# A graph layer on one core: engine order stated for 26 blocks only, an own bank for placed sums, two node banks, and the second block's additions moved up

## The chip, the cores and the metric

The kernel runs on one core of a Trainium2 chip. A core has five engines with a queue each: TensorE (PE, matmuls, with its weight loads shown as PEld), VectorE (DVE), ScalarE (ACT), GpSimd (POOL) and SyncE (SP). They run side by side and wait for each other through semaphores. Matmul results go to PSUM, which this kernel fills to its last bank[...]. The metric is device time in microseconds; lower is better. Times are medians over runs, and one execution was taken by the hardware profiler.

## The reference

A graph of 8192 nodes with 256 channels and 131072 edges with 64 attributes, everything in float32. Edges come sorted by destination. Reduced to what matters:

```python
ea  = edge_attr @ w_e + b_e                      # 131072 x 256
msg = relu(x[src] + ea)                          # a gather of rows of x
agg = segment_sum(msg, dst, 8192)
t   = x + agg
h_local = bn1(relu(t @ w1 + b1) @ w2 + b2 + x)
# attention within each graph of 32 nodes, 4 heads of 64 channels, on x
q, k, v = split(x.reshape(256, 32, 256) @ in_w.T + in_b)
h_attn  = bn2(softmax(q @ k.T / 8) @ v @ out_w.T + out_b + x)
out = h_local + h_attn
out = bn3(out + relu(out @ m_w1 + m_b1) @ m_w2 + m_b2)
return layernorm(x + out)
```

## The kernel before

**Edges** go in 128 blocks of 1024 (`NB`). For a block, `gather` (L124) issues eight indirect DMAs on the POOL queue, each fetching 128 rows of 256 channels into an `xs` tile; four such tiles exist, so the gathers of block b + 2 write the tile that the messages of block b - 2 read. The first `NX` blocks gather from x itself and add the bias `be` by extra matmuls (L468); later ones gather from `xb`, a copy of x with the bias in it, which `copy_load` and `copy_store` make during the first pairs. `load_edges` brings the attributes two blocks at a time. `edge_transpose` turns a block's attributes on TensorE into a `tp` tile, and ScalarE copies that to `eaT` (L169). `edge_products` multiplies `eaT` with `w_e` into two `pe` tiles of two banks each (L460). `edge_messages` adds `xs` to each on VectorE (L482) and takes relu on ScalarE (L486). `edge_hot` makes one-hot rows of the destinations (L491). `edge_sums` sums messages into windows by matmuls with them (`pw`, L505), copied by ScalarE (`ws`, L511). `edge_place` places the windows into node columns by another matmul (`l2`, L523) and VectorE adds the result to the chunk's `xT` (L533).

**Nodes** go in 16 chunks of 512 (`NCH`), and eight blocks feed one chunk. A chunk passes through three generators: `attention_front` (loads, transposes L283, q and k L294), `attention_back` (v L308, scores into two `pe` tiles L326, copied out by ScalarE L336, softmax on VectorE and ScalarE L342 to L353, then `oT` L361 and the output projection L373), and `dense` (four layers L392, transposes back L429, layer norm L434 to L442, store). Their matmuls write `at` tiles of one bank (`bank()`), evacuated by ScalarE or VectorE.

**PSUM** is shared out as three `at` banks, two `pe` tiles of two banks, and one bank with the tag `sm`, which `tp`, `pw` and `l2` use in turn.

**Order.** Blocks go in pairs until the last `NS` = 8, which go singly. Each pair's loop body issues edge steps, and between them calls `work.run(us)`. `Work` holds four streams of generators; a call takes steps from them in turn until the estimates they yield (1.7 for a layer step, 1.8 for scores, and so on) use up the given share of `per`, which is a number of blocks times `PER_X` or `PER`. A yield of `REST` keeps a stream out for the next call. A yield of `BEHIND` keeps it out until a call with `behind=True`, which is the pair's last, half of `per`, issued after the second block's messages: `attention_back` yields it ahead of the scores. Shares a stream can't use are kept only up to 2.0.

The whole edge loop stands in `tc.manual_schedule` (L609) for PE, DVE and ACT: each of these runs its instructions in the order in which the program states them. Outside such a block a planner lays out an engine's order itself when the program is built.

The order of a pair b, b + 1 in the loop: products b, messages b, window sums of the previous pair, products b + 1, node work (0.3 of `per`), the copy of x in early pairs, transposes of b + 2, work (0.1), placing, work (0.1), transposes of b + 3, one-hot rows of both, messages b + 1, work (0.5).

Of the kernel before, what the change touches and what calls it, by code (L numbers as in the profile page):

```python
# [9 lines left out]
FP = mybir.dt.float32  # L10
# [23 lines left out]
BPC = NB // NCH  # L34
TN = CH // P
GT = P // NPG
NX = 18
ND = 2
NS = 8
AGG_ROWS = N + 2 * P  # L40
TE = 8
RS = 1.0 / (1.0 + 1e-5) ** 0.5
LN_EPS = 1e-5

REST, BEHIND = -1.0, -2.0


VECS = ["b1", "b2", "bn1_g", "bn1_b", "in_b", "out_b", "bn2_g", "bn2_b", "m_b1", "m_b2", "bn3_g", "bn3_b"]
# [3 lines left out]
def gnn_kernel(ctx: ExitStack, tc: tile.TileContext, x, src, dst, edge_attr, w, out):  # L52
# [65 lines left out]
    pps = fast.enter_context(tc.tile_pool(name="fast_ps", bufs=1, space=PSUM))  # L118

    def bank():  # L120
        return pps.tile([P, CH], FP, name="at", tag="at", bufs=3)

    def bank2():
        return pps.tile([P, 2, CH], FP, name="pe", tag="pe", bufs=2)  # L124
# [176 lines left out]
    def attention_back(st, pool, bank, bank2):  # L301
        xT, hA, qk = st["xT"], st["hA"], st["qk"]
        vn = pool.tile([P, TN, C], FP, name="vn", tag="vn")
        for t0 in range(0, TN, 2):
            ps = bank()
            for t in range(t0, t0 + 2):
                for k in range(KC):
                    nc.tensor.matmul(  # L308
                        ps[:, (t - t0) * C : (t - t0 + 1) * C],
                        xT[:, k, t * P : (t + 1) * P],  # L310
                        inT[:, k, 2 * C :],
                        start=(k == 0),
                        stop=(k == KC - 1),
                    )
            nc.vector.tensor_copy(vn[:, t0 : t0 + 2, :].rearrange("p t c -> p (t c)"), ps)
            st["v"] = t0 + 2 == TN
            yield 1.7
        yield BEHIND

        pr = pool.tile([P, TN, H, NPG], FP, name="pr", tag="pr")  # L320
        for hh in range(H // 2):
            two = bank2()
            for t in range(TN):
                for s in range(2):
                    a = t * P
                    nc.tensor.matmul(  # L326
                        two[:, s, a : a + P],
                        qk[s * DH : (s + 1) * DH, hh, a : a + P],
                        qk[s * DH : (s + 1) * DH, KC + hh, a : a + P],
                        start=True,  # L330
                        stop=True,
                    )
            two4 = two.rearrange("p s (t k) -> p s t k", t=TN)
            for g in range(GT):
                q = slice(g * NPG, (g + 1) * NPG)
                nc.scalar.copy(pr[q, :, 2 * hh : 2 * hh + 2, :].rearrange("p t s k -> p s t k"), two4[q, :, :, q])  # L336
        st["scores"] = True
        yield 1.8
        prf = pr.rearrange("p t h k -> p (t h k)")
        pr3 = pr.rearrange("p t h k -> p (t h) k")  # L340
        mx = pool.tile([P, TN * H], FP, name="mx", tag="mx")
        nc.vector.tensor_reduce(mx, pr3, AX.X, ALU.max)  # L342
        nc.vector.tensor_sub(pr3, pr3, mx[:, :, None].to_broadcast([P, TN * H, NPG]))
        nc.scalar.activation(prf, prf, AF.Exp, scale=1.0 / DH**0.5)
        yield 0.0
        sm = pool.tile([P, TN * H], FP, name="sm", tag="sm")
        nc.vector.tensor_reduce(sm, pr3, AX.X, ALU.add)
        nc.vector.reciprocal(sm, sm)
        nc.vector.tensor_mul(pr3, pr3, sm[:, :, None].to_broadcast([P, TN * H, NPG]))

        for g in range(GT):
            q = slice(g * NPG, (g + 1) * NPG)
            nc.vector.transpose(bd[q, :, :, g, :].rearrange("p t h q -> p (t h) q"), pr3[q])  # L353
        yield REST
        oT = pool.tile([P, KC, CH], FP, name="oT", tag="oT")
        for k in range(KC):
            ps = bank()
            for t in range(TN):
                for s in range(2):
                    h = 2 * k + s  # L360
                    nc.tensor.matmul(  # L361
                        ps[s * DH : (s + 1) * DH, t * P : (t + 1) * P],
                        vn[:, t, h * DH : (h + 1) * DH],
                        bd[:, t, h].rearrange("p g q -> p (g q)"),
                        start=True,
                        stop=True,
                    )
            nc.scalar.activation(oT[:, k, :], ps, AF.Identity, bias=v_("in_b", 2 * KC + k))
        yield 1.8
        for o in range(KC):  # L370
            ps = bank()
            for k in range(KC):
                nc.tensor.matmul(  # L373
                    ps, outT[:, k, o * P : (o + 1) * P], oT[:, k, :], start=(k == 0), stop=(k == KC - 1)
                )
            nc.vector.scalar_tensor_tensor(
                hA[:, o, :], ps, s2[:, o : o + 1], hA[:, o, :], op0=ALU.mult, op1=ALU.add
            )
            st["done"] = o == KC - 1
            yield 1.7  # L380
# [135 lines left out]

    def edge_place(blocks, ws, oh2):

        l2 = pps.tile([P, KC, C], FP, name="l2", tag="sm", bufs=1)
        last = len(blocks) - 1  # L520
        for i in range(last + 1):
            for k in range(KC):
                nc.tensor.matmul(  # L523
                    l2[:, k, i * NPB : i * NPB + WB], ws[:, i, k * P : (k + 1) * P], oh2[:, i, :],
                    start=(i == 0 and k == 0), stop=(i == last), skip_group_check=True,
                )
        n = blocks[0] * NPB - WL
        end = n + last * NPB + WB
        for c in range(max(n, 0) // CH, (min(end, N) - 1) // CH + 1):
            assert chunk[c]["v"]  # L530
            a, z = max(n, c * CH), min(end, (c + 1) * CH)
            xT = chunk[c]["xT"][:, :, a - c * CH : z - c * CH]
            nc.vector.tensor_add(xT, l2[:, :, a - n : z - n], xT)  # L533
# [22 lines left out]
    class Work:  # L556
# [4 lines left out]

        def __init__(self, n):
            self.streams = [[] for _ in range(n)]
            self.rest, self.behind, self.turn, self.owed = [0] * n, [False] * n, 0, 0.0

        def add(self, stream, ready, gen):
            self.streams[stream].append((ready, gen))

        def may(self, i, behind):
            s = self.streams[i]  # L570
            return s and not self.rest[i] and (behind or not self.behind[i]) and s[0][0]()

        def run(self, us, behind=False):
            self.owed += us
            n, done = len(self.streams), 0
            self.rest = [max(r - 1, 0) for r in self.rest]
            while self.owed > 0:
                turns = [i % n for i in range(self.turn, self.turn + n)]
                i = next((i for i in turns if self.may(i, behind and done > 0)), None)
                if i is None:  # L580
                    i = next((i for i in turns if self.may(i, behind)), None)
                if i is None:
                    break
                if behind:
                    self.behind[i] = False
                t = next(self.streams[i][0][1], None)
                if t is None:
                    self.streams[i].pop(0)
                elif t == REST:
                    self.rest[i] = 2  # L590
                elif t == BEHIND:
                    self.behind[i] = True
                else:
                    self.owed -= t
                    done += t > 0
                    self.turn = (i + 1) % n
            self.owed = min(self.owed, 2.0)

        def finish(self):
            while any(self.streams):  # L600
                self.run(1e9, True)

    BACK, FRONT, DENSE, DENSE2 = range(4)
    work = Work(4)
    PER = 5.4
    PER_X = 4.5
    OTHER = ("vn", "qk", "oT", "pr", "o")
    placed = -1
    with tc.manual_schedule(engines={PE, mybir.EngineType.DVE, mybir.EngineType.Activation}):  # L609

        def last_of(c, t_z=TN):

# [21 lines left out]
        for i, c, t_a, t_z in (  # L634
# [6 lines left out]
                ready = lambda r=ready: r() and chunk[NCH - 1].get("done")  # L641
            work.add(i, ready, d)

        sums, waiting = None, []
        b = 0
        while b < NB:
            n = 2 if b < NB - NS else 1
            blocks, per = range(b, b + n), n * (PER_X if b < NX else PER)
            for i in blocks:
                if i % 2 == 0 and i + 4 < NB:  # L650
# [11 lines left out]
            waiting = list(blocks)  # L662
            if n == 2:
                edge_products(b + 1)
            if b == NB - 1:
                work.run(2.0)
                edge_place(*sums)
                placed = sums[0][-1]
                break
# [12 lines left out]
                    work.run(0.1 * per)  # L682
            for i in blocks:
                edge_hot(i)
            if n == 2:
                edge_messages(b + 1)
            work.run(0.5 * per, True)
            b += n
        edge_hot(NB - 1)
        work.run(1.5, True)  # L690
        sums = edge_sums(waiting)
        work.run(1.0, True)
        edge_place(*sums)
        placed = NB - 1
        work.finish()
# [124 lines left out]
```

## Time and profile before

| | |
|---|---|
| median of 3 runs | 1448.02 us (1444.78 to 1451.0) |
| profiled execution, device time | 1451.19 us |
| its span, first to last instruction | 1449.1 us |
| mean granted TensorE clock | 0.962 |
| gathers (POOL DMA_INDIRECT, three groups) | 1008, 952 to 994 ns each |
| moved by DMA | 206.77 MB, mean 143 GB/s |

How to read it: busy shares are averages over the span. A group's line in the profile gives the source line, the engine, the operation, what it writes and reads, and how often; after the bar stand its busy time, the mean of one, then the idle time of its engine right before it and what ended that idle time. "issue" is time in which an engine waited for nothing that the profile shows. fp32 matmuls appear in the trace as two instructions each.

From 569 to 1280 us the trace repeats one period of 88.5 to 89.2 us with 64 gathers, which is eight blocks and one chunk. Before that lie a start of 46 us with loads and set-up and a stretch in which the dense part has not yet begun or catches up; after it come the eight single blocks and the last dense steps.

In the trace, `pe<-DVE msg` in the list of waits means that PE stood idle before a matmul into a `pe` tile until the additions L482 ended.

### The profile page before, as it was taken

What the parts mean: (1) busy time and instruction counts of PE and PEld (TensorE: products, weight loads), DVE (VectorE), ACT (ScalarE), POOL (GpSimd) and SP (SyncE); (2) the same over time, 40 slices, a digit from 0 to 9 for tenths busy, and PEclk for the clock granted to TensorE, in tenths of its full rate; (3) what the DMA queues carried; (4) which work ended last, traced back from release to release, by engine and by line L of the source; (5) the groups of instructions that cost most, each with busy time, mean ns of one, the idle gap of its engine ahead of it and who ended that gap; (6) DMA issues with size and microseconds to landing.
All of it is one profiled execution on the core that took longest, in us unless ns stands there. A gap on an engine that the chain in (4) does not pass through costs nothing.

```text
span 1449.1 us, 21166 instructions
## 1 busy us (share of the span) xinstructions
PE 1268.8 (88%) x8275; PEld 795.4 (55%) x8275; DVE 709.4 (49%) x1202; ACT 658.3 (45%) x963; POOL 981.6 (68%) x1032
## 2 busy tenths in 40 slices
PE   5898999999999998988969799797997969888977
PEld 4566665555555655555545455454554545545645
DVE  5455635546463645354363543545345354454443
ACT  3434434545454554444444443453534545444433
POOL 7777757777777777775757667576775767757620
PEclk9998999999999999999989999999999999999999
DMA  8868544545454545453444534444444444434410
GB/s 288 293 196 258 184 137 135 164 118 163 134 148 130 162 133 148 127 157 95 134 128 130 158 101 134 137 130 139 124 127 132 135 130 129 135 109 136 118 53 17
DMA packets 140613, 206.77 MB, mean 143 GB/s; under 512 B 19646, under 2 KB 103900, under 8 KB 139740
## 3 DMA queue, kind: packets, MB, share of 16 engines
q0 software_dynamic: 49152, 134.28, 32.4%
q1 hardware_dynamic: 89468, 69.76, 15.3%
q8 instruction: 67, 1.10, 0.3%
q10 hardware_dynamic: 1888, 1.32, 0.3%
q14 instruction: 38, 0.31, 0.1%
HBM read 188.51 MB, written 16.78 MB: 142 GB/s over the span
## 4 chain that ended last, share of the span: by engine, by line
PE 52%; POOL 15%; DVE 14%; issue 9%; ACT 5%; DMA 5%; DVEq 0%; ACTq 0%; POOLq 0%
PE at L392 17%; POOL xs L134 15%; PE pe L460 12%; PE at L294 5%; DVE msg L482 5%; PE pw L505 4%; PE l L523 4%; PE at L373 3%; PE at L308 2%; PE tp L167 2%; DMA xs<-xb,srci 2%; ACT pr L336 2%; PE at L361 2%; DMA xs<-in_x_dram,srci 2%; DVE bd L353 1%
## 5 line engine op out<-in xcount | busy, mean ns | idle before, releaser
L134 POOL DMA_INDIRECT xs<-xb,srci x880 | 837.7, 952 | 361.6 <-issue 251.7
L486 ACT ACTIVATE msg<-msg 128x1024 f32<-128x1024 f32 (+1 forms) x258 | 267.0, 1051 | 234.9 <-DVE msg L482 230.1
L460 PE MATMUL pe<-we,eaT 64*128 64x256 f32 x2048 | 289.6, 422 | 80.5 <-DVE msg L482 44.5
L482 DVE TENSOR_TENSOR msg<-pe,xs 128x1024 f32<-128x1024 f32 (+1 forms) x258 | 302.1, 1209 | 104.8 <-ACT qk L297 34.2
L460 PEld LDWEIGHTS pe<-we,eaT 64*128 64x128 f32 x2048 | 202.8, 203 | 171.8 <-DVE msg L482 57.1
L169 ACT COPY eaT<-tp 128x512 f32<-128x512 f32 x128 | 74.3, 581 | 198.2 <-PE tp L167 197.9
L134 POOL DMA_INDIRECT xs<-in_x_dram,srci x128 | 127.2, 994 | 42.0 <-issue 35.9
L505 PE MATMUL pw<-msg,oh 128*32 128x256 f32 x2048 | 128.2, 390 | 0.0
L533 DVE TENSOR_TENSOR xT<-l,xT 128x352 f32<-128x352 f32 (+4 forms) x98 | 43.1, 465 | 170.1 <-PE l L523 169.8
L392 PE MATMUL at<-hA,mw 128*128 128x512 f32 (+2 forms) x304 | 125.0, 539 | 1.3 <-DVE hA L402 0.9
L294 PE MATMUL at<-xT,inT 128*128 128x512 f32 x256 | 122.2, 602 | 0.0
L392 PE MATMUL at<-m,mw 128*128 128x512 f32 (+2 forms) x304 | 116.7, 526 | 0.0
L167 PEld LDWEIGHTS tp<-ident,ea 128*128 128x128 f32 x512 | 61.9, 143 | 89.6 <-issue 48.2
L167 PE MATMUL tp<-ident,ea 128*128 128x128 f32 x512 | 80.4, 281 | 33.2 <-DVE xT L533 19.2
L523 PE MATMUL l<-oh,ws 128*128 128x160 f32 x512 | 84.9, 307 | 27.1 <-ACT eaT L169 26.1
L523 PEld LDWEIGHTS l<-oh,ws 128*128 128x128 f32 x512 | 73.7, 190 | 47.2 <-ACT eaT L169 34.5
L408 ACT ACTIVATE m<-at,vec 128x512 f32<-128x512 f32 (+2 forms) x76 | 46.9, 619 | 104.8 <-PE at L392 104.5
L505 PEld LDWEIGHTS pw<-msg,oh 128*32 128x32 f32 x2048 | 60.4, 112 | 60.2 <-issue 28.2
L417 DVE SCALAR_TENSOR_TENSOR zT<-at,s,zT 128x512 f32<-128x512 f32 (+2 forms) x38 | 25.3, 667 | 119.1 <-PE at L392 116.8
L392 PEld LDWEIGHTS at<-m,mw 128*128 128x128 f32 x304 | 54.7, 190 | 45.5 <-issue 42.0
L297 ACT ACTIVATE qk<-at,vec 128x512 f32<-128x512 f32 x64 | 44.0, 687 | 78.5 <-PE at L294 78.4
L392 PEld LDWEIGHTS at<-hA,mw 128*128 128x128 f32 x304 | 53.5, 195 | 46.7 <-issue 38.7
(109 smaller groups left out, 1336.0 us busy)
## 6 DMA issues: line engine op xcount, KB each, us to landing
ea<-in_edge_attr_dram SPq DMA_DIRECT2D x64, 512.0 KB
xs<-xb,srci POOLq DMA_INDIRECT x880
xn<-in_x_dram SPq DMA_DIRECT2D x16, 512.0 KB
out_dram<-y SPq DMA_DIRECT2D x14, 512.0 KB
xp<-in_x_dram SPq DMA_DIRECT2D x10, 512.0 KB
xb<-xp SPq DMA_DIRECT2D x10, 512.0 KB
xp<-in_x_dram SPq DMA_DIRECT2D x3, 1024.0 KB
xb<-xp SPq DMA_DIRECT2D x3, 1024.0 KB
```

The costliest lines, as they stand in the source:

```text
L134: nc.gpsimd.indirect_dma_start(out=xs[:, h, j, :], out_offset=None, in_=x if b < NX else xb[:, :], in_offset=bass.IndirectOffsetOnAxis(ap= ...
L167: nc.tensor.transpose(tp[:, h, :], ea[:, h, :], ident)
L169: nc.scalar.copy(eaT, tp)
L294: nc.tensor.matmul(ps, inT[:, k, o * P : (o + 1) * P], xT[:, k, :], start=(k == 0), stop=(k == KC - 1))
L297: nc.scalar.activation(qk[:, o, :], ps, AF.Identity, bias=v_("in_b", o))
L392: nc.tensor.matmul(ps, wt[:, k, o * P : (o + 1) * P], act[:, k, :], start=(k == 0), stop=(k == nk - 1))
L408: nc.scalar.activation(m1[:, o, :], layer(mw1, KC, o, hA), AF.Relu, bias=v_("m_b1", o))
L460: nc.tensor.matmul(pe[:, i, u, :], eaT[rows, h + u, :], we[rows, :], start=(b >= NX or u == 0), stop=(b >= NX), skip_group_check=True,)
L482: nc.vector.tensor_add(msg[:, hs].rearrange("p u i c -> p i u c"), pe[:, :, u : u + n, :], xs[:, hs].rearrange("p u i c -> p i u c"),)
L486: nc.scalar.activation(msg[:, hs], msg[:, hs], AF.Relu)
L505: nc.tensor.matmul(pw[h * WN : (h + 1) * WN, i, :], oh[:, h * TJ + j, :], msg[:, h, j, :], start=(j == 0), stop=(j == TJ - 1), skip_group_ ...
L523: nc.tensor.matmul(l2[:, k, i * NPB : i * NPB + WB], ws[:, i, k * P : (k + 1) * P], oh2[:, i, :], start=(i == 0 and k == 0), stop=(i == la ...
```

## The change

It does these things:

- `edge_place` writes a tile of its own tag `l2`, one bank; `bank()` has two `at` banks instead of three. PSUM stays full.
- `edge_messages(b + 1)` is issued right behind `edge_products(b + 1)`, ahead of the pair's first node work, instead of after the one-hot rows.
- `BEHIND` and all that serves it in `Work` are gone: scores may stand in any share of a pair.
- The stated order of DVE and ACT ends when b reaches `NV` = 26; PE's is stated throughout.
- `NX` goes from 18 to 20, `PER` from 5.4 to 5.1, `PER_X` from 4.5 to 4.2.

Both programs have the same number of instructions on DVE, POOL and SP's data moves; PE has 16 more matmuls (the bias of two blocks), and ACT's order holds 24 table loads where it held 28, counted over the whole program.

```diff
-NX = 18
+NX = 20
 ND = 2
+NV = 26
...
-REST, BEHIND = -1.0, -2.0
+REST = -1.0
...
     def bank():
-        return pps.tile([P, CH], FP, name="at", tag="at", bufs=3)
+        return pps.tile([P, CH], FP, name="at", tag="at", bufs=2)
...
             st["v"] = t0 + 2 == TN
             yield 1.7
-        yield BEHIND
...
-        l2 = pps.tile([P, KC, C], FP, name="l2", tag="sm", bufs=1)
+        l2 = pps.tile([P, KC, C], FP, name="l2", tag="l2", bufs=1)
...
-        def may(self, i, behind):
+        def may(self, i):
             s = self.streams[i]
-            return s and not self.rest[i] and (behind or not self.behind[i]) and s[0][0]()
-
-        def run(self, us, behind=False):
+            return s and not self.rest[i] and s[0][0]()
+
+        def run(self, us):
             self.owed += us
-            n, done = len(self.streams), 0
+            n = len(self.streams)
             self.rest = [max(r - 1, 0) for r in self.rest]
             while self.owed > 0:
                 turns = [i % n for i in range(self.turn, self.turn + n)]
-                i = next((i for i in turns if self.may(i, behind and done > 0)), None)
-                if i is None:
-                    i = next((i for i in turns if self.may(i, behind)), None)
+                i = next((i for i in turns if self.may(i)), None)
...
-    PER = 5.4
-    PER_X = 4.5
+    PER = 5.1
+    PER_X = 4.2
...
-    with tc.manual_schedule(engines={PE, mybir.EngineType.DVE, mybir.EngineType.Activation}):
+    with tc.manual_schedule(engines={PE}):
...
+        early = ExitStack()
+        early.enter_context(tc.manual_schedule(engines={mybir.EngineType.DVE, mybir.EngineType.Activation}))
         sums, waiting = None, []
         b = 0
         while b < NB:
             n = 2 if b < NB - NS else 1
+            if b == NV:
+                early.close()
...
             if n == 2:
                 edge_products(b + 1)
+                edge_messages(b + 1)
...
             for i in blocks:
                 edge_hot(i)
-            if n == 2:
-                edge_messages(b + 1)
-            work.run(0.5 * per, True)
+            work.run(0.5 * per)
```

More of the change, by code (lines that the diff above doesn't have):

```diff
@@ L563, in __init__ @@
             self.streams = [[] for _ in range(n)]
-            self.rest, self.behind, self.turn, self.owed = [0] * n, [False] * n, 0, 0.0
+            self.rest, self.turn, self.owed = [0] * n, 0, 0.0
         def add(self, stream, ready, gen):
             self.streams[stream].append((ready, gen))
-        def may(self, i, behind):
+        def may(self, i):
             s = self.streams[i]
-            return s and not self.rest[i] and (behind or not self.behind[i]) and s[0][0]()
-        def run(self, us, behind=False):
+            return s and not self.rest[i] and s[0][0]()
+        def run(self, us):
             self.owed += us
-            n, done = len(self.streams), 0
+            n = len(self.streams)
             self.rest = [max(r - 1, 0) for r in self.rest]
@@ L578, in run @@
                 turns = [i % n for i in range(self.turn, self.turn + n)]
-                i = next((i for i in turns if self.may(i, behind and done > 0)), None)
-                if i is None:
-                    i = next((i for i in turns if self.may(i, behind)), None)
+                i = next((i for i in turns if self.may(i)), None)
                 if i is None:
                     break
-                if behind:
-                    self.behind[i] = False
                 t = next(self.streams[i][0][1], None)
@@ L590, in run @@
                     self.rest[i] = 2
-                elif t == BEHIND:
-                    self.behind[i] = True
                 else:
                     self.owed -= t
-                    done += t > 0
                     self.turn = (i + 1) % n
@@ L600, in finish @@
             while any(self.streams):
-                self.run(1e9, True)
+                self.run(1e9)
     BACK, FRONT, DENSE, DENSE2 = range(4)
     work = Work(4)
-    PER = 5.4
-    PER_X = 4.5
+    PER = 5.1
+    PER_X = 4.2
     OTHER = ("vn", "qk", "oT", "pr", "o")
     placed = -1
-    with tc.manual_schedule(engines={PE, mybir.EngineType.DVE, mybir.EngineType.Activation}):
+    with tc.manual_schedule(engines={PE}):
         def last_of(c, t_z=TN):
@@ L684, in gnn_kernel @@
                 edge_hot(i)
-            if n == 2:
-                edge_messages(b + 1)
-            work.run(0.5 * per, True)
+            work.run(0.5 * per)
             b += n
         edge_hot(NB - 1)
-        work.run(1.5, True)
+        work.run(1.5)
         sums = edge_sums(waiting)
-        work.run(1.0, True)
+        work.run(1.0)
         edge_place(*sums)
```

## The prediction

> **What bounds the kernel now.** I read the page's busy shares first, then busy time by stretch, then the timeline of one stretch, then the list of waits. On the page:
>
> ```profile
> PE 1268.8 (88%) x8275; PEld 795.4 (55%) x8275; DVE 709.4 (49%) x1202; ACT 658.3 (45%) x963; POOL 981.6 (68%) x1032
> L134 POOL DMA_INDIRECT xs<-xb,srci x880 | 837.7, 952 | 361.6 <-issue 251.7
> ```
>
> TensorE is the busiest, but the gathers come close: one takes 0.95 us and the next starts 0.30 us later even when nothing holds it, so eight (one block) need 10.0 us and all 1008 need 1264 us. TensorE and the gathers are near-equal bounds; vector and scalar engines have half their time free and matter by the place where they make the others wait.
>
> Busy time by stretch (columns: PE, PE weight loads, DVE, ACT, POOL, clock, DMA share, GB/s):
>
> ```profile
> 480.00:569.00 89.00, 81.84 (x586) 50.56 (x582) 50.71 (x88) 49.06 (x73) 67.67 (x71) 1.00 0.52 151
> ...
> 746.70:835.50 88.80, 76.74 (x488) 46.33 (x488) 42.03 (x71) 40.93 (x58) 60.78 (x64) 0.96 0.45 131
> ```
>
> From about 569 to 1280 us the kernel repeats one period of 88.9 us, eight blocks (one node chunk), eight times. In it POOL does 64 gathers where 71 fit, PE idles 12.1 us, and the clock is 0.96. Before that, 71 gathers went into 89 us and PE idled 7. One period's bubble, from the timeline:
>
> ```profile
> 818.57 2.29 PE L326 MATMUL pe<-qk 64*128 64x128 f32 x32 [0.21 <-DVE msg L482]
> 823.21 2.98 ACT L336 COPY pr<-pe 32x256 f32<-32x256 f32 x8
> 824.74 1.31 PE L460 MATMUL pe<-we,eaT 64*128 64x256 f32 x8 [3.87 <-ACT pr L336]
> 831.41 2.85 DVE L353 STREAM_TRANSPOSE bd<-pr 32x512 f32<-32x512 f32 x4
> 834.29 2.36 DVE L482 TENSOR_TENSOR msg<-pe,xs 128x1024 f32<-128x1024 f32 x2
> 835.57 3.60 PE L460 MATMUL pe<-we,eaT 64*128 64x256 f32 x16 [5.05 <-DVE msg L482]
> 836.91 0.97 POOL L134 DMA_INDIRECT xs<-xb,srci  x1 [7.13 <-DVE oh L514]
> ```
>
> The scores (L326) stand last before the next pair's products and use the same two pe tiles: PE waits 3.87 us for ScalarE to copy them out. VectorE then works off the whole softmax in its stated order (826.2 to 834.3) before the additions (L482) that free the next pe tile: 5.05 us more. Those additions also free the gather's buffer, so POOL stands 7.13 us. Together with a 0.20 us remnant this is 9.1 us a chunk. The third leak is the sm bank, which transposed edges, window sums and placed sums share:
>
> ```profile
> PE l L523 <- ACT eaT L169: 26.1, 34, 1.2
> PE tp L167 <- DVE xT L533: 19.2, 20, 2.1
> ```
>
> 45.3 us over the run, 2.4 us in a period (0.82 + 0.73 + 0.87 in its timeline).
>
> **The change part by part.**
>
> **Own bank for the placed sums.** Takes the two waits above away: up to 45 us over the run, of which 2.4 x 8 = 19 in the eight periods. The transposes still share with the window sums; that wait (PE tp behind ACT ws, 7.8 us) stays, all of it in the single blocks at the end.
>
> **Two node banks instead of three.** The trace holds no wait for a third bank, so I bound it. A layer group is 1.72 us on PE (L392 x4) and its evacuation 0.69 (ACT) or 0.75 (DVE) plus about 0.25 of hand-over: with two banks the third group finds its bank free if the evacuating engine comes within 0.7 us. Below: nothing. Above: where short groups follow each other (L283 x8 in 1.04 us, L429 x8 likewise) PE waits for the first evacuation, 0.5 to 1 us each, and once a chunk a second-layer group's evacuation (L376, L402) stands in VectorE's queue behind four stream transposes (2.85) and additions (2.36), some 2 us. I take 3.5 of 0 to 6 us a chunk. Here a rule weighs: the Trainium skill, "Perfetto Trace Analysis", "Identifying Performance Opportunities", reads a bubble that repeats as possibly too few buffers in PSUM. By it, taking a node bank away should deepen the bubble: 12 us a chunk would stay or grow, 1450 or more. The row says otherwise: the bubble stands at pe, whose two tiles are unchanged, and is ended by an engine's order (DVE msg behind bd), not by a missing third tile. I follow the row and keep the rule for the other side.
>
> **Second block's additions right behind its products.** Two L482 and two relu a pair move forward; no DMA of their own moves. Their end frees pe and a gather buffer: in the trace products end at 788.8 and these additions start at 796.3, so 7.5 us earlier. POOL, held only in the bubble, gains where that buffer was the one it lacked. Past them now wait the first evacuations of the pair: two relu, 2.2 us, in front of ACT's first node evacuation. The first group needs 1.72 us to be ready and its bank is wanted two groups later, so this fits with some 0.3 us to spare; it is in the 3.5.
>
> **No more holding scores back.** In the changed program's PE order scores no longer stand last in their pair; output transposes (1.04), a layer group or two (1.72 each), or an edge transpose and placing stand between. The trace before prices such cover: in 302 to 569 us, where layer work followed the scores, PE waited 3.4 us in all behind the copies (L336) and not once behind DVE msg. That is the 3.87 gone.
>
> **VectorE and ScalarE free after block 26.** In the built order most chunks have the additions inside the softmax (max, subtract, addition, sum, ..., addition), but two or three have reductions, multiply and all four stream transposes ahead of them. By the trace's durations (copies 2.98, two steps of 0.69, table load 1.28 and exp 0.63, three steps 1.65, transposes 2.85) and the PE work in front of the next products, PE is held from 0.6 us (best) to about 5 (worst); I take 3 a chunk. Table loads fall from 28 to 24 in the order of the whole program, 4 x 1.28 = 5 us of ScalarE time beside other work: no time.
>
> **Blocks 18 and 19 from x, smaller shares.** Two more blocks with the be product (L468 x8 in 0.95 us, twice a block: 1.9 us): +3.7 us of PE. POOL's longest single stop, 8.96 us at 201.8 where gathers turn to xb, should vanish: the copy gets 20 us more. Shares of 5.1 and 4.2 instead of 5.4 and 4.5 leave later chunks work the earlier ones did: from the order, the dense part lags about three pairs at block 50 and two at block 92. I price it 1.6 us a chunk (8 x 5.1 against 39.4 units, at 45.8 us of node work per 39.4 units).
>
> **The sum.** A period at present: 76.7 busy, 12.1 idle. After: the slow clock costs 3.5 us of the 76.7 now (products in 3.60 instead of 2.00, 1.31 + 2.08 instead of 2.00); half goes with the long gaps: 75.0. Plus 1.6. Plus idle: banks 3.5, softmax 3, chunk start behind xT 0.5, rest 0.5, together 7.5. That is 84.1, above POOL's 80.3, so PE sets it: 4.8 x 8 = 38 us saved. Between 302 and 569 us there was no bubble to remove: the 26.3 blocks there (420 matmuls at L460, 16 a block) at 76.6 / 8 busy and 7.5 / 8 idle make 277 against 267: 10 lost. Between 46 and 302: POOL's stops of 13.5 and the sm waits of 12.8 against 3.7 of extra products: the gathers bound the gain at 13.5, and I take 8. After 1280: sm waits 4.4 and 5.5 behind DVE msg, less 3 for banks: 7 saved. Net 43: 1451.2 (the profiled execution, span 1449.1 plus 2.1 around it) becomes 1408. The median of the runs, 1448.0, lies 3 lower: **1405**.
>
> **The rivals.**
> **POOL bounds it** (0.13): banks cost nothing and the free order keeps additions in front. Then 80.3 to 81.5 a period, 60 to 68 saved there, and 10 to 15 elsewhere: about 1368. For it: the stretch 480 to 569 ran so. Against: the chunks with all transposes in front.
> **Bubble only moves** (0.08): softmax before additions in nearly every chunk, 5 us, banks 4: 86.8 a period, 17 saved, given back between 302 and 569. About 1443. Against: the order shows it for the minority.
> **Head-of-queue stall with two banks** (0.21, slower): the free order was laid out for durations other than the trace's. An addition that waits at VectorE's head for its gather, or a sum waiting 2 us for exp (DVE sm behind ACT pr, 25.2 us in all now, the worst 2.3), holds every node evacuation behind it; with two banks PE stops after two groups, 3.4 us, where three gave 5.2. It decides once idle time passes about 10 us per eight blocks from block 26 on, against my 7.5; at 13 the period is 89.6 (+6 in all), 302 to 569 loses 28, the gains at both ends shrink to nothing: about 1480. For it: POOL and PE are within 5% of each other, so gathers land just in time.
>
> **Numbers.** My forecast has 0.58 (idle 5 to 10 per eight blocks: 1370 to 1441). What a measurement can tell from no change is about 0.5%, 7 us. Faster 0.71 (forecast nearly whole, POOL case), same 0.08, slower 0.21. Range 1362 to 1462: the POOL case in its middle, the forecast, and the slower case up to its first half.
>
> **What would show it.** Right: PE's waits for ACT eaT and DVE xT at l and tp nearly gone; waits of pe products for ACT pr under 10 us; POOL's longest stops under 5 us; period 82 to 86; clock near 0.98. New lines: at groups waiting for DVE or ACT evacuations, about 3.5 us a chunk. Wrong: PE at waits beyond 6 us a chunk, DVE msg waiting on xs with PE idle at at, or a period still with one gap of over 5 us at pe.

## The result, and the profile after

The changed kernel takes **1332.26 us** (median of 4 runs, 1331.56 to 1332.57) against 1447.41 for the kernel before in the same session (4 runs, 1444.78 to 1451.0): a ratio of **0.9202, 95% interval 0.9182 to 0.9223**. That is 115 us less, where 43 were forecast; the time lies below the range and also below the rival in which the gathers bound the kernel (1368).

The page of the changed kernel: busy times, POOL in 40 slices, and the groups of the gathers from `xb` and of the products:

```profile
PE 1234.3 (93%) x8307; PEld 783.6 (59%) x8307; DVE 712.2 (54%) x1202; ACT 658.7 (49%) x959; POOL 983.9 (74%) x1032
...
POOL 7777777777777777777777777777777777777770
...
L134 POOL DMA_INDIRECT xs<-xb,srci x864 | 824.9, 955 | 263.8 <-issue 249.8
...
L459 PE MATMUL pe<-we,eaT 64*128 64x256 f32 x2048 | 262.3, 391 | 12.0 <-DVE msg L481 11.1
```

The same row and the group of the products in the kernel before:

```profile
POOL 7777757777777777775757667576775767757620
...
L460 PE MATMUL pe<-we,eaT 64*128 64x256 f32 x2048 | 289.6, 422 | 80.5 <-DVE msg L482 44.5
```

Before, POOL's row was 7 but for one slice up to about 650 us (a slice is 36.2 us) and then 5, 6 and 7 by turns; now it is 7 in every slice but the last. One gather takes 0.95 us and the next follows 0.30 us later, which is 76% busy, so "7 everywhere" means that the gathers never stop. The difference in the time at which the last gather ends, 1392.1 against 1299.8 us, is POOL's stops. Its waits (us in total, times, longest), the two largest beside the list's `issue`, which is the 0.30 us behind each gather; kernel before:

```profile
POOL xs L134 <- DVE oh L514: 67.9, 12, 7.4
POOL xs L134 <- DVE msg L482: 30.0, 21, 2.7
```

and after:

```profile
POOL xs L134 <- DVE oh L513: 3.8, 6, 1.7
...
POOL xs L134 <- DVE msg L481: 2.4, 8, 0.3
```

With the single stop of 9.0 us where gathers turned to `xb`, which is gone too, 107 us have become 6; without the 0.30 us that stand in each of these stops in any case, 97 have become 2.

On the other side of the bubble stands PE. Its two largest waits before:

```profile
PE pe L460 <- DVE msg L482: 44.5, 9, 5.5
PE pe L460 <- ACT pr L336: 35.9, 16, 3.9
```

and after, the two largest and what is left behind the copies:

```profile
PE pe L459 <- DVE msg L481: 11.1, 13, 3.6
PE at L360 <- DVE bd L352: 10.4, 2, 7.1
...
PE pe L459 <- ACT pr L335: 0.7, 1, 0.7
```

The copies that PE waited for before the products (L336, now L335) hold it only once, for 0.7 us; transposed edges and placed sums no longer wait for each other's bank (PE tp behind xT is gone, PE l behind eaT as well). What is left is spread over many small waits, most of them at `at`.

By stretch (columns as before: us, PE, PE weight loads, DVE, ACT, POOL, clock, DMA share, GB/s), two of the periods after:

```profile
542.00:622.00 80.00, 75.21 (x492) 46.07 (x491) 41.62 (x72) 39.67 (x57) 60.50 (x65) 0.98 0.50 144
...
862.00:942.00 80.00, 73.76 (x498) 45.32 (x497) 43.25 (x74) 41.32 (x60) 60.51 (x65) 1.00 0.50 145
```

64 or 65 gathers stand in every 80 us, while PE is busy for 73.4 to 78.0 of them (mean 75.3 over nine such stretches). POOL's count is the constant, PE's varies, and VectorE's additions now wait for rows to land, which cost 3.9 us in the kernel before:

```profile
DVE msg L481 <- DMA xs<-xb,srci: 23.6, 13, 6.0
```

So the gathers set the period.

Where the 118.4 us of span went, from the end of the n-th gather in both traces. There are 1024 gathers in each program, eight for each of 128 blocks; the 1008 given earlier lack the first 16, which have their indices from another tile (`srcd`).

| up to | before, us | after, us | saved in between |
|---|---|---|---|
| gather 208 | 282.1 | 272.5 | 9.6 |
| gather 448 | 587.0 | 575.0 | 2.4 |
| gather 960 (eight periods) | 1302.5 | 1219.7 | 70.8 |
| gather 1024, the last | 1392.1 | 1299.8 | 9.5 |
| end of span | 1449.1 | 1330.7 | 26.1 |

The last row had no term in the forecast. What is left to do when the last gather has ended, before:

```profile
1392.10:1449.10 57.00, 42.04 (x292) 31.88 (x292) 21.98 (x51) 19.52 (x41) 0.01 (x1) 0.95 0.04 13
```

and after:

```profile
1299.80:1330.70 30.90, 22.88 (x170) 17.46 (x168) 12.72 (x35) 9.91 (x25) 0.00 (x0) 0.94 0.07 24
```

Before, three of the four `xs` buffers still wait for their products when the gathers end (48 matmuls at L460), and 42 us of PE are left in all. After, PE has followed the gathers so closely that one block's products (16 matmuls) and 23 us of PE remain. **Work that waits in buffers because PE is late is paid once more at the end**; with PE no longer late it is gone.

The same saving counted on PE: idle time falls from 180.3 to 96.4 us (83.9), busy time from 1268.8 to 1234.3 (34.5), though the bias of two more blocks was added. 27.3 us of the latter are the products alone (289.6 before, 262.3 now, 2048 matmuls each). At the 2.00 us that a block's 16 take where nothing held PE up, they would need 256: of 33.6 us above that, 6.3 are left. Most of the difference is the clock. In the bubble of the kernel before, the 16 products behind the wait of 5.05 us ran at a granted clock of 0.53 (the columns above, for instructions on `pe` tiles alone; no POOL):

```profile
835.57:839.20 3.63, 3.60 (x16) 2.40 (x16) 1.08 (x1) 0.00 (x0) 0.53 0.13 36
```

and products after, with no wait before them, at full clock:

```profile
553.54:555.54 2.00, 2.00 (x16) 1.46 (x16) 0.00 (x0) 0.00 (x0) 1.00 0.37 102
```

In all runs of the section on the experiments except one (`b_seven`, an eighth of the gathers taken from the kernel before), the kernel before itself took 2113 to 2181 us instead of its ordinary 1447, at a granted clock of 0.82 to 0.84, so each of those ratios is of that condition and none of them divides up the 115 us.

### The profile page after: what moved, and what is told of

Read it like the earlier page. It is cut to its first block, busy times and chain, and to the rows that moved or that the text cites. A ratio compares the mean times of both kernels' runs of the same rounds, so it can differ in the third digit from the quotient of the medians.

```text
span 1330.7 us, 21178 instructions
## 1 busy us (share of the span) xinstructions
PE 1234.3 (93%) x8307; PEld 783.6 (59%) x8307; DVE 712.2 (54%) x1202; ACT 658.7 (49%) x959; POOL 983.9 (74%) x1032
## 4 chain that ended last, share of the span: by engine, by line
PE 56%; POOL 17%; issue 9%; DVE 8%; ACT 6%; DMA 4%; DVEq 0%; ACTq 0%; POOLq 0%
POOL xs L134 17%; PE at L391 16%; PE pe L459 11%; PE at L294 6%; PE pw L504 5%; PE l L522 3%; PE at L372 3%; DVE msg L481 3%; PE at L308 3%; PE tp L167 3%; PE pe L467 3%; DMA xs<-xb,srci 2%; PE at L360 2%; ACT pr L335 2%; DVE bd L352 1%
## 5 line engine op out<-in xcount | busy, mean ns | idle before, releaser
L134 POOL DMA_INDIRECT xs<-xb,srci x864 | 824.9, 955 | 263.8 <-issue 249.8
L485 ACT ACTIVATE msg<-msg 128x1024 f32<-128x1024 f32 (+1 forms) x258 | 270.9, 1051 | 329.5 <-DVE msg L481 320.7
L459 PE MATMUL pe<-we,eaT 64*128 64x256 f32 x2048 | 262.3, 391 | 12.0 <-DVE msg L481 11.1
L459 PEld LDWEIGHTS pe<-we,eaT 64*128 64x128 f32 x2048 | 187.3, 187 | 99.7 <-issue 43.5
L134 POOL DMA_INDIRECT xs<-in_x_dram,srci x144 | 142.1, 987 | 45.3 <-issue 41.1
L504 PE MATMUL pw<-msg,oh 128*32 128x256 f32 x2048 | 124.6, 382 | 0.0
L504 PEld LDWEIGHTS pw<-msg,oh 128*32 128x32 f32 x2048 | 59.6, 109 | 54.6 <-issue 21.9
L522 PE MATMUL l<-oh,ws 128*128 128x160 f32 x512 | 81.8, 301 | 0.5 <-ACT ws L510 0.5
L294 PEld LDWEIGHTS at<-xT,inT 128*128 128x128 f32 x256 | 46.1, 192 | 50.2 <-issue 47.2
L391 PE MATMUL at<-xT,w 128*128 128x512 f32 (+2 forms) x152 | 64.8, 558 | 10.1 <-DVE y L431 4.7
L391 PE MATMUL at<-h,w 128*128 128x512 f32 (+2 forms) x152 | 65.5, 554 | 9.1 <-ACT h L398 6.4
```

What stands on the lines that cost most here:

```text
L134: nc.gpsimd.indirect_dma_start(out=xs[:, h, j, :], out_offset=None, in_=x if b < NX else xb[:, :], in_offset=bass.IndirectOffsetOnAxis(ap= ...
L294: nc.tensor.matmul(ps, inT[:, k, o * P : (o + 1) * P], xT[:, k, :], start=(k == 0), stop=(k == KC - 1))
L391: nc.tensor.matmul(ps, wt[:, k, o * P : (o + 1) * P], act[:, k, :], start=(k == 0), stop=(k == nk - 1))
L459: nc.tensor.matmul(pe[:, i, u, :], eaT[rows, h + u, :], we[rows, :], start=(b >= NX or u == 0), stop=(b >= NX), skip_group_check=True,)
L485: nc.scalar.activation(msg[:, hs], msg[:, hs], AF.Relu)
L504: nc.tensor.matmul(pw[h * WN : (h + 1) * WN, i, :], oh[:, h * TJ + j, :], msg[:, h, j, :], start=(j == 0), stop=(j == TJ - 1), skip_group_ ...
```

## What the trace of the changed kernel tells by itself

Two things could have removed the bubble at `pe`: the free VectorE order, which may put additions inside the softmax, or the smaller shares and the lifted rule on scores, which let layer matmuls stand between the scores and the next products. The changed kernel does both, but its trace holds chunks in which only the second was at work. From block 26 on there are twelve chunks. In five the built order has the whole softmax and all four transposes ahead of the additions, as the stated order of the kernel before had. One of them (start us, us, engine, line, operation; in brackets the idle time before and what ended it):

```profile
863.35 2.06 PE L325 MATMUL pe<-qk 64*128 64x128 f32 x32
...
865.83 3.60 PE L391 MATMUL at<-xT,w 128*128 128x512 f32 x8
...
872.10 1.12 PE L391 MATMUL at<-h,w 128*128 128x512 f32 x2 [1.70 <-ACT h L398]
873.15 2.00 PE L459 MATMUL pe<-we,eaT 64*128 64x256 f32 x16
873.93 2.84 DVE L352 STREAM_TRANSPOSE bd<-pr 32x512 f32<-32x512 f32 x4
876.80 2.36 DVE L481 TENSOR_TENSOR msg<-pe,xs 128x1024 f32<-128x1024 f32 x2
878.08 2.27 PE L459 MATMUL pe<-we,eaT 64*128 64x256 f32 x16 [1.07 <-DVE msg L481]
```

The additions come nearly as late behind the scores as before (13.4 us from the scores' start to the end of the transposes, against 15.7), but the products come 7.7 us after the scores' end, not directly behind the copies, so PE loses 1.07 us where it lost 3.87 and 5.05. In the other seven, additions stand inside the softmax:

```profile
547.92 2.06 PE L325 MATMUL pe<-qk 64*128 64x128 f32 x32
...
549.91 3.70 PE L391 MATMUL at<-m,mw 128*128 128x512 f32 x8
...
553.54 2.00 PE L459 MATMUL pe<-we,eaT 64*128 64x256 f32 x16
...
556.47 1.22 DVE L481 TENSOR_TENSOR msg<-pe,xs 128x1024 f32<-128x1024 f32 x1
557.61 0.69 DVE L352 STREAM_TRANSPOSE bd<-pr 32x512 f32<-32x512 f32 x1
557.74 1.13 PE L459 MATMUL pe<-we,eaT 64*128 64x256 f32 x8 [0.34 <-DVE msg L481]
```

Here one layer group of the last layer, 3.7 us long, covers the copies, and the additions, slipped in ahead of the transposes, release the second products after 0.34 us. Over all twelve chunks:

| chunks | products after the scores' end | additions | longest wait for them |
|---|---|---|---|
| five (scores at 408, 483, 863, 941, 1020 us) | 7.7 to 18.1 us | behind the whole softmax | 1.07 us |
| seven (316, 548, 627, 709, 784, 1092, 1169) | 3.3 to 5.8 us | inside it | 0.89 us |
| before, eight (640 to 1263) | 3.9 us, all of it waiting | behind the whole softmax | 5.5 us |

So cover of 3.3 us or more behind the scores removes the wait for the copies everywhere, and in five chunks longer cover removes the wait for the additions too. In the seven with short cover the additions stand inside the softmax. That this is the work of the free order can't be read from this trace; the stated order of the same program, in the next section, has them behind the whole softmax in only two of the seven.

## The experiments

Each run gives its own time and that of the kernel before on the same chip. The times expected are for a kernel before of about 1450 us; but for one run below they can't be set against what was measured, and the ratios, the orders and the waits are what is left to read. Of the kernel before itself there is no trace in that condition.

### Stated order to the end

```diff
-NV = 26
+NV = 1000
...
         work.finish()
+        early.close()
```

> The kernel after, but VectorE and ScalarE keep the stated order to the end of the edge loop. If the free order is what removes the bubble (theory F): softmax stands ahead of the additions again, PE waits 4 to 9 us a chunk at pe, POOL stops again, 1390 to 1430. If moving the second block's additions up and letting scores stand anywhere is enough (theory M): POOL stays without stops over 3 us and the time is 1330 to 1350. If the own bank carries it (theory B): no more than 1345 either, so this run tells F from the other two.

> The kernel after with VectorE and ScalarE stated to the end, once more, because on the chip of the first runs the kernel before itself took 2161 us against 1447 and every engine but POOL stopped for long stretches that no instruction of the program explains. Theory F (the free order removes the bubble): 1390 to 1430 where before takes some 1447. Theory M (additions up, scores anywhere): 1330 to 1350, POOL without stops.

> The kernel after with VectorE and ScalarE stated to the end, where before takes about 1450 us. Theory F (the free order removes the bubble): 1390 to 1430, POOL stops of 4 to 8 us once a chunk. Theory M (additions up, scores anywhere): 1330 to 1350, POOL without stops over 3 us.

Measured: 2079.89 against 2160.98 (0.967, interval 0.961 to 0.973), 2015.81 against 2123.4 (0.949, 0.944 to 0.955), 2078.25 against 2158.97 (0.965, 0.958 to 0.972). From the list of PE's waits of the third:

```profile
PE pe L459 <- DVE msg L481: 11.5, 7, 4.1
PE pe L459 <- ACT pr L335: 9.8, 3, 5.2
```

All the rest of the change, without the free order, keeps a gain of 3 to 5%, and the waits at `pe` are as small as those of the unchanged after-kernel in the same condition (11.5 and 11.3, below). So there the free order was not what removed them.

These runs also show what the stated order is. PE's order is the same, instruction for instruction, as in the changed kernel. Of the seven chunks with short cover, five have the additions ahead of the softmax's maximum or between its steps even as stated, because additions and scores now stand elsewhere in their pair. One of them, from the third run:

```profile
893.49 1.23 DVE L481 TENSOR_TENSOR msg<-pe,xs 128x1024 f32<-128x1024 f32 x1 [0.19 <-PE at L428]
...
894.63 0.68 DVE L341 TENSOR_REDUCE mx<-pr 128x16 f32<-128x512 f32 x1
```

In the other two (709 and 784 us in the table above) they stand behind the whole softmax, and there PE does wait for them:

```profile
1128.17 2.85 DVE L352 STREAM_TRANSPOSE bd<-pr 32x512 f32<-32x512 f32 x4
1131.05 2.35 DVE L481 TENSOR_TENSOR msg<-pe,xs 128x1024 f32<-128x1024 f32 x2
...
1132.33 1.22 PE L459 MATMUL pe<-we,eaT 64*128 64x256 f32 x4 [4.11 <-DVE msg L481]
```

The three runs agree: 4.1 to 4.5 us in the first of the two chunks and 1.9 to 2.3 in the second, where the unchanged kernel in the same condition shows none. So within the whole change the free order has two chunks of the last twelve to mend. What that is worth in time in the ordinary condition was not measured.

### The free order alone

```diff
+NV = 26
...
-    with tc.manual_schedule(engines={PE, mybir.EngineType.DVE, mybir.EngineType.Activation}):
+    with tc.manual_schedule(engines={PE}):
...
+        early = ExitStack()
+        early.enter_context(tc.manual_schedule(engines={mybir.EngineType.DVE, mybir.EngineType.Activation}))
...
+            if b == NV:
+                early.close()
```

on the kernel before, nothing else changed.

> The kernel before with only the stated order of VectorE and ScalarE ended at block 26; additions of the second block late, three node banks, placed sums in the shared bank. F: additions slip in between the steps of the softmax, the 5.05 us gap at pe goes, POOL's stops fall under 3 us, 1340 to 1380. M: the scores still stand last before the next products, so PE still waits some 4 us for the copies, and the additions are still late: 1410 to 1445. B: 1410 to 1445.

> The kernel before with only the stated order of VectorE and ScalarE ended at block 26, where before takes about 1450 us. F: 1340 to 1380, no gap at pe over 4 us. M and B (the own bank for placed sums): 1410 to 1445.

Measured: 2029.9 against 2160.98 (0.942, 0.937 to 0.947) and 2025.89 against 2158.97 (0.940, 0.934 to 0.945). PE's waits of the first (lines shifted by 2):

```profile
PE pe L461 <- ACT pr L337: 36.5, 14, 5.8
...
PE tp L168 <- DVE xT L534: 27.3, 14, 4.5
...
PE pe L461 <- DVE msg L483: 6.1, 8, 2.1
```

With the free order only 6.1 us behind the additions are left (5.2 in the second run), against 57.7 in the next experiment, whose order is stated. The wait for the copies (36.5) and the waits at the shared bank (27.3 at tp, 24.5 at l) stay. So added to the kernel before, the free order takes the wait for the additions, but not that for the copies.

### Additions moved up and scores let loose, order stated

```diff
-        yield BEHIND
...
             if n == 2:
                 edge_products(b + 1)
+                edge_messages(b + 1)
...
-            if n == 2:
-                edge_messages(b + 1)
```

on the kernel before, with its shares of 5.4 and 4.5, three node banks and the shared bank.

> The kernel before with only the second block's additions moved up behind their products and scores no longer held back; stated order throughout, three node banks, shared bank, old shares. M: cover stands between scores and the next products, PE waits at pe fall from 80 us to under 25 and POOL's stops under 3 us: 1340 to 1370. F: the softmax still stands ahead of the next pair's first additions: 1400 to 1440. B: the shared bank's 45 us stay: 1400 or more.

> The kernel before with only the second block's additions moved up and scores no longer held back, where before takes about 1450 us. M: 1340 to 1370. F: 1400 to 1440, because the softmax still stands ahead of the next pair's first additions. B: 1400 or more, with the 45 us of waits at l and tp.

Measured: 2116.06 against 2160.98 (0.982, 0.977 to 0.987) and 2110.61 against 2158.97 (0.978, 0.974 to 0.982), the smallest gain of all. PE's waits of the second:

```profile
PE pe L459 <- DVE msg L481: 57.7, 12, 7.1
...
PE pe L459 <- ACT pr L335: 28.2, 10, 8.2
```

The bubble stands. In this run's PE order, from the seventh chunk on, only eight output transposes stand between the scores and the next products, although nothing holds the scores back any more; in the kernel after, the last twelve chunks have at least one layer group there. **Lifting the rule and moving the additions do not bring the layer groups behind the scores by themselves.** That the smaller shares do it is an argument, not shown: there is no run of the kernel after with the old shares.

### Three node banks, placed sums back in the shared bank

```diff
-        return pps.tile([P, CH], FP, name="at", tag="at", bufs=2)
+        return pps.tile([P, CH], FP, name="at", tag="at", bufs=3)
...
-        l2 = pps.tile([P, KC, C], FP, name="l2", tag="l2", bufs=1)
+        l2 = pps.tile([P, KC, C], FP, name="l2", tag="sm", bufs=1)
```

on the kernel after.

> The kernel after with three node banks and the placed sums back in the shared bank. B: the 45 us of waits at l and tp come back and the gathers are held: 1360 to 1385. M and F: POOL sets the end, and PE has a few us of slack a chunk: 1330 to 1345, with PE waits at l and tp of 30 to 45 us hidden for the most part.

Measured: 2054.98 against 2160.98 (0.955, 0.950 to 0.960). PE's waits:

```profile
PE tp L167 <- DVE xT L532: 125.1, 26, 17.1
PE l L522 <- ACT eaT L169: 93.2, 21, 20.9
```

The waits at the shared bank come back, and become the largest of that list; the waits at `pe` stay small (14.4 behind the additions). So the own bank removes these two, and the rest of the change does not. Beside the unchanged after-kernel (next but one), which ran on another chip, the ratio is 0.955 against 0.947 with touching intervals: what it is worth in time can't be told here.

### One gather in eight replaced

```diff
+                if h == NH - 1 and j == TJ - 1:
+                    nc.sync.dma_start(xs[:, h, j, :], x[b * P % N : b * P % N + P, :])
+                    continue
```

in the loop that issues a block's gathers: 896 gathers are left; the eighth tile of each block is loaded as 128 rows in order through SP, so those messages are made from other nodes' rows. It is done to the kernel before and to the kernel after.

> The kernel before with the last of the eight gathers of each block replaced by a plain load of 128 consecutive rows of x from SP's queue (those messages use other rows and, from block 18 on, lack the bias). If before was held by its own order and not by the gathers' rate, taking an eighth of the gathers' 1285 us away leaves it where it is: 1430 to 1450 where before takes 1447. If the gathers' rate bounded it: 1330 or less.

> The kernel after, but the last of the eight gathers of each block is replaced by a plain load of 128 consecutive rows of x from SP's queue, so 896 gathers are left (those messages use other rows and, from block 20 on, lack the bias). If the gathers bound the kernel after (1299.8 us of its 1330.7 end with the last gather, none stops over 2 us): the gathers need 1124 us, PE becomes the bound with 1234 us of work and 50 to 60 of idle time, and the time falls to 1280 to 1300. If PE bounds it and the gathers merely fit: no change, 1325 to 1340. If the plain loads are slow in coming: above.

> The kernel after with one gather in eight replaced by a plain load of 128 consecutive rows, where before takes about 1450 us. Gathers bound after: the time falls to 1280 to 1300, where PE's 1234 us of work and some 50 to 60 of idle take over. PE bounds it: 1325 to 1340.

On the kernel **before**: 1453.76 against 1450.06, ratio **1.003 (1.001 to 1.005)**, at the ordinary condition, just above the 1430 to 1450 expected if the gathers were not the bound. An eighth of POOL's gathers, 128 x 1.25 = 160 us of its pace, taken away, and nothing gained. POOL's largest stop and, below it, one stretch (lines shifted by 3):

```profile
POOL xs L137 <- DVE msg L485: 156.6, 49, 5.9
```

```profile
746.70:835.50 88.80, 77.90 (x492) 46.73 (x490) 42.33 (x71) 41.03 (x59) 53.08 (x56) 0.94 0.45 131
```

The same 88.8 us hold 56 gathers where they held 64, and POOL just stands longer, behind the additions that free its buffers. Its stops before were consequences of PE's bubble, not the cause: PE with its waits bound the old kernel.

On the kernel **after**: 1940.61 against 2148.77 (0.904, 0.897 to 0.911) and 1941.01 against 2158.97 (0.901, 0.896 to 0.907), where the unchanged kernel, on another chip, has 0.947. This does not show that the gathers bind: POOL was busy for only 44% of the span in the second of these runs and stood still for 633 us behind the additions, so the gain there has another cause, which these runs don't show. That the gathers bind the changed kernel in the ordinary condition rests on its own trace: from 3.3 to 1299.8 us, 1024 gathers at 0.95 + 0.30 fill 1282 of 1296.5 us. The run that would test it, fewer gathers in the ordinary condition, is missing.

### The kernel after again, beside these runs

> The kernel after, unchanged, as the measure for the other runs on chips where before takes over 2100 us. Where before takes about 1450: 1330 to 1336. Where it takes over 2100, all theories: faster than every part of it alone (0.94 of before with the free order alone), so 0.90 to 0.94.

Measured: 2011.64 against 2126.38, ratio 0.947 (0.935 to 0.960), not 0.920, and above the 0.90 to 0.94 expected here. Two of PE's waits:

```profile
PE pe L459 <- DVE msg L481: 11.5, 12, 2.6
PE pe L459 <- ACT pr L335: 11.3, 8, 6.5
```

The changed kernel gains in this condition too, but less, and the bubble at `pe` is gone here as there. Set beside it, the stated order (0.949 to 0.967), the free order alone (0.940, 0.942), and three banks (0.955) lie within two per cent, so the whole is not faster here than its parts: they don't add up, and several of them reach the same place. The ratio also depends on the chip (the stated order has 0.949 on one and 0.965 and 0.967 on two others), so a hundredth between runs on different chips says nothing.

## Why the prediction was wrong in size

The direction and most of the mechanism were right: the waits that were to go went. What bounds the kernel afterwards was wrong, and the sum was 75 us short: the traced span it meant was 1406 (1408 less the 2.1 around it), measured 1330.7. By its steps:

| step of the prediction | forecast | measured |
|---|---|---|
| scores' cover takes the wait for the copies (3.87 a chunk) | gone | gone: 0.7 us in the whole run |
| own bank takes tp and l waits | gone, but for 7.8 behind ACT ws | gone; 2.3 behind ACT ws and a new 3.5 behind eaT at tp |
| two node banks | 3.5 us a chunk | at most 2.4: 12.0 us of waits at `at` in five periods, and 6.2 more that are for the matmul's own input |
| free order: softmax holds the products | 3 a chunk | 0.8 a chunk |
| slow clock of a period's products | half of 3.5 goes | nearly all of it |
| PE in a period, busy and idle | 76.6 and 7.5 | 75.8 and 4.8 |
| eight periods | 84.1 each, PE sets them, 38 saved | 80.6 each, the gathers set them, 70.8 saved |
| 302 to 569 us | 10 lost | 2.4 saved |
| 46 to 302 us | 8 saved | 9.6 saved, POOL's stop of 8.96 gone |
| after 1280 us | 7 saved | 35.6 saved (9.5 + 26.1) |

**The step that failed** is the comparison in the sum: "That is 84.1, above POOL's 80.3, so PE sets it". The terms on PE's side were too large, the idle ones above all (4.8 us where 7.5 were summed). *Softmax, 3*: a chunk with all reductions and transposes in front of the additions was priced at about 5 us, but the five of that kind lose 1.07 at most, because PE has other work meanwhile. In the one shown, the first addition ends 12.6 us after the scores, and PE's other work in between (transposes, layer groups, the first products, sums) with its own waits fills 11.6 of them. *The clock*: "half goes with the long gaps", but the slow products (3.60 us instead of 2.00, and 1.31 + 2.08) stood behind the gaps of 3.9 to 5.5 us at `pe`, and with no such gap left hardly a slow product is: 27 us of PE time in the run. (The two readings beside the 3.5 make 3.0.) The granted clock rose from 0.962 to 0.986, as the forecast's test line (near 0.98) had it, without that line's being carried into the sum. *The lag of the dense part, 1.6*, can't be seen apart; PE's busy time in a period is 75.8 us (75.3 in 80), where 75.0 + 1.6 were summed. How much less time than the gathers PE would need by itself can't be read off; that they never stop says that it is not more. The gathers' own floor was also counted short: 1024 of them, not 1008, need 1282 us.

**The term that was missing** is the tail, 26 us, for which the sum had only waits ("7 saved"). Once the gathers set the pace, two of the three blocks that waited in the buffers at the end are gone. The rival "POOL bounds it" had the right mechanism, with "80.3 to 81.5 a period, 60 to 68 saved there, and 10 to 15 elsewhere", and missed by 36 us for the same reason: its sum ended at the last period. For the same cause "302 to 569: 10 lost" fell: PE's time was counted where gathers, 71 in 89 us before, already set the pace, and they cannot be slowed by a PE that has time to spare.

**Two node banks** cost what was forecast or a little less. A late evacuation of the kind named, behind the transposes and additions of a chunk, is seen in the trace after, though for the output transposes (`y`) and not for a second-layer group:

```profile
559.43 2.14 DVE L352 STREAM_TRANSPOSE bd<-pr 32x512 f32<-32x512 f32 x3
...
562.28 2.35 DVE L481 TENSOR_TENSOR msg<-pe,xs 128x1024 f32<-128x1024 f32 x2
...
565.28 1.34 PE L391 MATMUL at<-xT,w 128*128 128x512 f32 x2 [3.66 <-DVE y L431]
```

The rival that made this the bound asked for about 10 us of idle time per eight blocks; PE idles 4.8 in 80. The rule that the prediction weighed, as it used it, would have kept the period at 88.9 or above; the bubble went although a node bank was taken away, as the row (`DVE msg` behind `bd`, at a tile whose count didn't change) had said. The rule itself is not refuted: PE did wait for a free `pe` tile, and a third one was not tried.

**Left open**: how much of the 92 us up to the last gather each part brings at the ordinary condition, above all the free order, which has two chunks to mend by the stated runs; and the test that fewer gathers make the changed kernel faster there.

## What to carry to other kernels

When two resources lie within a few per cent of each other, work out the floor of the second one as a whole, start and end included: here 3 us of start, 1024 gathers at 1.25 us, some 15 us of longer gathers and stops, and the tail of 31 are the whole 1331. A bubble costs more than its idle time: it also costs the slow clock of the work behind it, and, at the end of the kernel, the work that piled up in the buffers meanwhile. To see whether an engine's stated order is harmful, look first at what else that waiting engine has to do in the meantime: 3.3 us of other matmuls behind the scores removed one wait completely, and 8 us of them left 1.07 us of the next with the softmax as far ahead as before.

## What the hardware showed that was not expected

The condition of the experiments: the kernel before took 2113 to 2181 us on several chips, and 1450 on one of these at another time. POOL's gathers kept their 0.95 + 0.30 us, and busy times of VectorE and ScalarE did not change (709.7 and 661.1 us when the kernel after ran there, 712.2 and 658.7 in the first run). But PE, busy for 1442.0 of 2001.3 us, idled for 559 instead of 96. In front of the window sums alone it stood 52 times, 40.1 us in all, for nothing that the profile shows (`PE pw L504 <- issue: 40.1, 52, 1.7`; no such wait in the first run), and work that needs a matmul's result could begin late. In the first run with the order stated to the end:

```profile
900.67 0.60 PE L167 MATMUL tp<-ident,ea 128*128 128x128 f32 x4
...
905.00 0.59 ACT L169 COPY eaT<-tp 128x512 f32<-128x512 f32 x1 [2.58 <-PE l L522]
```

The transposes in `tp` end at 901.3 by the trace and ScalarE, free since 902.4, copies them at 905.0. What causes the condition was not found.

In the ordinary condition, the clock's recovery was a surprise in size: identical instructions, 2048 product matmuls, took 289.6 us of PE in one order of the program and 262.3 in the other.
